# A graph layer on one core: rows in a ring of 66 tiles instead of six buffers, asked for earlier, and their places turned and spread at other times

## The chip, the cores and the metric

The kernel runs on one core of one Trainium2 chip. The metric is device microseconds of one launch. Before the change the median of three runs is 5410.82 us (5407.89 to 5411.46).

## The reference, cut to what matters

The reference is one attention layer over a graph of 12,500 nodes (128 features) and 412,500 edges, sorted by their second node, around a layer norm and a residual:

```python
h = relu(layernorm(x))
hmid = leaky_relu(concat([q[src], k[tgt], eh]) @ A1 + b1, 0.2)      # q, k, v from h; eh from the edge's 64 features
scores = leaky_relu(hmid @ A2 + b2, 0.2)                            # 8 heads
w = softmax(scores.mean(-1), axis=0)                                # over all edges
out = segment_sum(w[:, None] * v[tgt], src, num_segments=num_nodes)
y = x + gamma * normalize(h @ Wn + bn + out) + beta
```

The sum goes to the edge's first node (src), while the edges are sorted by the second. So each edge's row must be brought from one order into the other.

## The kernel before

**Chunks and blocks.** The edges are cut into four chunks (403 groups of 1024 edges: 121, 109, 98 and 75 groups). The nodes are cut into 98 blocks by their first node. In each chunk a block has room for a fixed number of tiles of 128 edges: 11, 10, 9 and 7. Tiles are worked on in quads of up to four, three quads for a block of the first three chunks, two for one of the last.

**First pass** (`first_stage`). For each group, SP loads the edge features, a window of the k and v table, and the edges' offsets in it (L769, L774, L777). Four times a group PE makes two tiles of rows (L809, L812), ACT copies them into a ring of 16 rows with their place in front (L792, L795), and POOL scatters each tile of 128 rows of 257 floats with an indirect DMA (L747) to the block's slots in a table in HBM. Two such tables are used in turn.

**Second pass** (`second_stage`). It goes through the blocks of the chunk before, in steps counted as half steps, two for each quad. For a block whose first quad is turned at half step t:

- `load` (L834, L837): SP loads the block's rows (tiles x 128 x 257 floats) into one of six buffers of 11 tiles, and the block's q rows (qw, five buffers). The time comes from `load_at`: 17 half steps ahead of t with three quads, 11 with two, but not before the block six earlier has been multiplied.
- `places` (L841): PE transposes the column of places into the PSUM bank t_bank. `put_places` (L846, L848), one half step later: ACT copies it to plT and stores it to HBM (pl_d). `spread_places` (L854): SP loads it back to all 128 partitions (pls, two buffers). With three quads these come at t - 9, t - 8 and t - 6, with two at t - 8, t - 7 and t - 5.
- `select` (L861): DVE makes sel_q from pls at t - 1. `turn` (L870, L873): PE transposes the rows and adds the node's q rows by sel_q. `steep` (L881, L882): ACT and DVE apply the leaky relu. `heads_of` to `exponentials` (L889 to L943): heads, scores, running maximum and weights.
- `weights` (L955) and `products` (L964), eleven half steps (LAG) after t: DVE makes a weighted selection for each tile and PE multiplies it with the v part of the rows into o_ps; `add_sums` (L973) adds that to the sums.

**What sets the order.** The program order of PE, DVE, ACT and SP is written out by hand. `at(when, turn, job)` puts each job into a half step and a rank in it. `interleave` mixes the first pass of a chunk with the second pass of the chunk before in proportion to their numbers of steps: 588 half steps in each of the first two mixtures, 594 in the third, and 414 of the last chunk alone behind it. The first pass of chunk 0 runs ahead of them with the work on the nodes. Each engine works in its order, so an instruction that waits holds all that stand behind it; SP's queue carries all loads.

I call the mixtures stages 1, 2 and 3 and the last chunk's second pass stage 4. At the start of each, the first load of rows waits until the last scatter of the chunk has landed.

Of the kernel before, what the change touches and what calls it, by code (L numbers as in the profile page):

```python
# [10 lines left out]
FP = mybir.dt.float32  # L11
# [3 lines left out]
U8 = mybir.dt.uint8  # L15
# [7 lines left out]
P = 128  # L23
# [10 lines left out]
QUAD = 4  # L34
LAG = 11

BUFS = 6

RROWS = 16

# [10 lines left out]
ROW = 2 * D + 1  # L51
# [18 lines left out]
def interleave(*jobs):  # L70

    jobs = [[g, max(n, 1), 0] for g, n in jobs]
    while jobs:
        job = min(jobs, key=lambda j: (j[2] + 0.5) / j[1])
        try:
            next(job[0])
            job[2] += 1
        except StopIteration:
            jobs.remove(job)


def some_steps(job, n):

    for _ in range(n):
        next(job, None)
        yield
# [25 lines left out]
def kernel(ctx: ExitStack, tc: tile.TileContext, n_edges, x, src, dst, ea, w_nv, w_qt, w_kt,  # L112
# [12 lines left out]
    nc = tc.nc  # L125
# [17 lines left out]
    most_tiles = max(ct for _, _, ct, _ in chunks)  # L143

    blocks = []
# [25 lines left out]
    def clear_ends(c):  # L171

        ct = chunks[c][2]
        k = min(SPARE, ct)
        for b in range(NTN):
            nc.sync.dma_start(out=tabs[c % 2][(b * ct + ct - k) * P:(b + 1) * ct * P, :].rearrange("(p j) r -> p (j r)", p=P),
                             in_=blank[:, 0:k * ROW])
            yield
# [13 lines left out]
    first = once.tile([P, P], FP, name="first")  # L192
# [225 lines left out]
    def clear_rest(c):  # L418

        ct = chunks[c][2]  # L420
        rest = ct - min(SPARE, ct)
        if rest > 0:
            turns = nc.values_load(trips[0:1, c:c + 1], min_val=0, max_val=NTN, skip_runtime_bounds_check_because=BECAUSE)
            with tc.For_i(0, turns, 1) as b:
                for j in range(rest):
                    nc.sync.dma_start(out=tabs[c % 2][ds(b * (ct * P) + j * P, P), :], in_=blank[:, 0:ROW])
# [84 lines left out]
    def ready(c):  # L511

        yield from count(c)
        yield from plan(c)
        yield from place_slots(c)

    def ready_steps(c):
        nt = chunks[c][1] * SUPER
        return _ceil(nt, 5 * STR) + 4 + 2 * _ceil(nt, STR)

    def ready_enough():

        return ready_steps(0) - 2 * _ceil(chunks[0][1] * SUPER, STR) + 2 * 2 * 8 + 1
# [146 lines left out]
    main = ctx.enter_context(ExitStack())  # L670
# [153 lines left out]
    def second_stage():  # L824


        rows_of, qws, plss, state = {}, {}, {}, {}
        state["s_ps"] = ps_s.tile([P, 512], FP, name="s_ps")
        nc.vector.memset(state["s_ps"], 0.0)

        def load(i):
            c, b, ct, _, _ = blocks[i]
            rows_of[i] = pb.tile([P, most_tiles, ROW], FP, name="rows_of")
            nc.sync.dma_start(out=rows_of[i][:, 0:ct, :],  # L834
                              in_=tabs[c % 2][b * ct * P:(b + 1) * ct * P, :].rearrange("(p j) r -> p j r", p=P))
            qws[i] = ps.tile([P, 3 * D], BF, name="qw")
            nc.sync.dma_start(out=qws[i], in_=q_tab.rearrange("(p t) d -> t p d", p=P)[b])  # L837
# [4 lines left out]

        def put_places(i):
            ct = blocks[i][2]
            plT = p3.tile([most_tiles, P], U8, name="plT")
            nc.scalar.activation(plT[:ct, :], t_bank[:ct, 0:P], AF.Copy)  # L846
            at = i % 4 * most_tiles
            nc.scalar.dma_start(out=pl_d[at:at + ct, :], in_=plT[:ct, :])  # L848
# [129 lines left out]
        def at(when, turn_, job, *args):  # L978
            plan_of.setdefault(when, []).append((turn_, len(plan_of[when]) if when in plan_of else 0, job, args))

        for i, (c, b, ct, nq, i0) in enumerate(blocks):
            t = 2 * i0
            at(load_at(i), 2, load, i)
            first = t - 9 if nq > 2 else t - 8
            at(first, 3, places, i)
            at(first + 1, 0, put_places, i)
            at(first + 3, 0, spread_places, i)
            at(t - 1, 3, select, i)
            for q in range(nq):
                at(t + 2 * q, 1, turn, i, q)  # L990
                at(t + 2 * q + 1, 0, steep, i, q)
            t += 2 * nq
            at(t - 1, 3, heads_of, i)
            at(t, 0, add_bias, i)
            at(t + 1, -1, by_slot, i)
            at(t + 1, -1, scores, i)
            at(t + 2, 2, spread_top, i)
            at(t + 2, 3, greatest, i)
            at(t + 3, 2, exponentials, i)
            at(t + 4, 3, add_weights, i)  # L1000
            t = 2 * i0 + LAG
            for q in range(nq):
                at(t + 2 * q - 1, 0, weights, i, q)
                at(t + 2 * q, 1, products, i, q)
            at(t + 2 * nq - 1, 0, add_sums, i)
        for when in range(min(plan_of), max(plan_of) + 1):
            for _, _, job, args in sorted(plan_of.get(when, []), key=lambda j: j[:2]):
                job(*args)
            yield

    def load_at(i):

        _, _, _, nq, i0 = blocks[i]
        t = 2 * i0 - (17 if nq > 2 else 11)
        if i >= BUFS:
            _, _, _, nq, i0 = blocks[i - BUFS]
            t = max(t, 2 * (i0 + nq - 1) + LAG)
        return t

    def all_sums():  # L1020

# [8 lines left out]
    def count_left():  # L1030

        nc.tensor.matmul(t_bank[:, 0:1], lhsT=ones, rhs=left, start=True, stop=True)
        nc.vector.tensor_scalar(trips[:, NC:NC + 1], t_bank[0:1, 0:1], 0.0, float(NG), op0=ALU.is_gt, op1=ALU.mult)

    def other_edges(most_of):

        with tc.tile_pool(name="others", bufs=1) as op, tc.tile_pool(name="others_ps", bufs=1, space=PSUM) as ops_:
            turns = nc.values_load(trips[0:1, NC:NC + 1], min_val=0, max_val=NG, skip_runtime_bounds_check_because=BECAUSE)
            with tc.For_i(0, turns, 1) as g:  # L1039
# [71 lines left out]
                with tc.For_i(0, NTN, 1) as b:  # L1111
# [8 lines left out]
                    nc.vector.tensor_add(a, a, bank[:, 0:D])  # L1120

    second = second_stage()
    ends = [load_at(c * NTN) for c in range(NC)]
    ends.append(2 * (blocks[-1][4] + blocks[-1][3]) + LAG)
    for c in range(NC + 1):
        jobs = []
        if c == NC:
            count_left()
        else:
            if c == 0:  # L1130
                clear_rest(c)
            jobs.append((first_stage(c), chunks[c][1] * halves))
        if c > 0:
            n = ends[c] - ends[c - 1]
            jobs.append((some_steps(second, n), n))
        if c == 0:
            jobs.append((chain(first_ready, ready(1)), ready_steps(0) - ready_enough() + ready_steps(1)))
        elif c + 1 < NC:
            jobs.append((ready(c + 1), ready_steps(c + 1)))
        if c + 1 < 2:  # L1140
            jobs.append((clear_ends(c + 1), NTN))
        if c == 0:
            with tc.manual_schedule(engines={ET.PE, ET.DVE, ET.Activation, ET.SP}):
                interleave(*jobs)
                for _ in node_steps:
                    pass
            clear_rest(1)
            setup.close()
            pb = main.enter_context(tc.tile_pool(name="pb", bufs=BUFS))
            ps = main.enter_context(tc.tile_pool(name="ps", bufs=5))  # L1150
            pw = main.enter_context(tc.tile_pool(name="pw", bufs=8))
            p3 = main.enter_context(tc.tile_pool(name="p3", bufs=1))
            ps_h = main.enter_context(tc.tile_pool(name="ps_h", bufs=2, space=PSUM))
            ps_s = main.enter_context(tc.tile_pool(name="ps_s", bufs=1, space=PSUM))
            ps_o = main.enter_context(tc.tile_pool(name="ps_o", bufs=1, space=PSUM))
        else:
            with tc.manual_schedule(engines={ET.PE, ET.DVE, ET.Activation, ET.SP}):
                interleave(*jobs)
# [88 lines left out]
```

## Time and profile before

| | us |
|---|---|
| median of three runs | 5410.82 (5407.89 to 5411.46) |
| the profiled execution | 5393.0 |
| its span, first to last instruction | 5391.3 |
| busy PE, DVE, ACT, POOL | 4218.1, 4204.3, 2160.8, 3379.1 |
| mean granted clock of TensorE | 0.921 |

| stage | what runs | us of the span | scatters |
|---|---|---|---|
| start and first pass of chunk 0 | nodes, places, scatters | 0 to 1455 | 968 |
| 1 | first pass of chunk 1, second of chunk 0 | 1456 to 2664 | 872 |
| 2 | first pass of chunk 2, second of chunk 1 | 2668 to 3765 | 783 |
| 3 | first pass of chunk 3, second of chunk 2 | 3770 to 4686 | 599 |
| 4 | second pass of chunk 3 | 4690 to 5299 | none |
| end | normalization and output | 5299 to 5391 | none |

How to read the lines of the profile below: PE is the matrix engine and PEld its weight loads; DVE, ACT, POOL and SP are the vector, scalar, GpSimd and sync engines; SPq is SP's queue of DMA issues. A line of waits, "A <- B: x, n, m", says that A stood idle for x us in n cases, at most m us, until B released it. A line of a timeline has the start, the duration, the engine, the line of the kernel and what is written from what. A DMA's duration there is the time to issue it, not to move the data.

### The profile page before, as it was taken

How to read it: one execution, taken by the hardware profiler on the slowest of the kernel's cores; microseconds unless marked ns; L12 is line 12 of the kernel's file. 1: busy time of each engine (PE TensorE's matmuls, PEld its weight loads, DVE VectorE, ACT ScalarE, POOL GpSimd, SP SyncE). 2: the span in 40 equal slices, each digit the busy share in tenths (PEclk: the TensorE clock that was granted, in tenths of full speed). 3: DMA queues.
4: the chain of work that ended last, by engine and by line, in shares of the span. 5: the costliest groups of instructions: out<-in, count | busy, mean ns of one | idle time of the engine just before them, and what ended most of it. 6: DMA issues, size and time to landing. Idle time of an engine off the chain costs nothing. (4 is left out here: it accounts for less than half of the span.)

```text
span 5391.3 us, 90152 instructions
## 1 busy us (share of the span) xinstructions
PE 4218.1 (78%) x26817; PEld 2951.6 (55%) x27160; DVE 4204.3 (78%) x13299; ACT 2160.8 (40%) x6046; POOL 3379.1 (63%) x3261
## 2 busy tenths in 40 slices
PE   4777766565588888998788888987888888878782
PEld 2344433333266666666566666665666666655551
DVE  7777754544378888888788988887877788799889
ACT  1344422222244444444344444443444444434333
POOL 0477777777677777777667777777666666500002
PEclk8788887777789999999999999999999999999996
DMA  8677765555489999888789999988899998755554
GB/s 244 201 234 228 230 196 162 169 164 167 162 262 290 280 280 282 279 281 281 251 257 284 289 284 282 282 286 260 263 284 280 276 287 284 242 194 193 190 194 164
DMA packets 609678, 1309.97 MB, mean 243 GB/s; under 512 B 117392, under 2 KB 371524, under 8 KB 571168
## 3 DMA queue, kind: packets, MB, share of 16 engines
q1 hardware_dynamic: 404312, 841.81, 53.1%
q0 software_dynamic: 154704, 424.26, 21.8%
q10 hardware_dynamic: 50168, 38.07, 2.2%
q8 instruction: 218, 3.57, 0.3%
q14 instruction: 276, 2.26, 0.1%
HBM read 782.14 MB, written 521.60 MB: 242 GB/s over the span
## 5 line engine op out<-in xcount | busy, mean ns | idle before, releaser
L747 POOL DMA_INDIRECT tab<-row,slots x3223 | 3343.9, 1038 | 1339.5 <-issue 702.8
L809 PE MATMUL row_ps<-w_ea,ea_t 128*128 128x256 f32 x3224 | 1105.0, 427 | 379.2 <-ACT row L795 311.5
L964 PE MATMUL o_ps<-rows_of,w 128*128 128x128 f32 x7252 | 1073.6, 287 | 127.9 <-DVE w L955 125.7
L964 PEld LDWEIGHTS o_ps<-rows_of,w 128*128 128x128 f32 x7252 | 954.8, 193 | 254.7 <-DVE w L955 199.7
L795 ACT ACTIVATE row<-row_ps 128x512 f32<-128x512 f32 x1612 | 939.6, 590 | 279.7 <-PE row_ps L812 215.7
L955 DVE TENSOR_SCALAR w<-iota_f,rows_of,score 128x128 f32<-128x128 f32 x3626 | 1037.2, 356 | 0.8 <-ACT score L938 0.8
L809 PEld LDWEIGHTS row_ps<-w_ea,ea_t 128*128 128x128 f32 x3224 | 577.9, 208 | 680.9 <-ACT row L795 397.7
L881 ACT ACTIVATE low<-h_ps 128x512 f32<-128x512 f32 (+3 forms) x1078 | 569.0, 528 | 848.7 <-PE h_ps L873 690.8
L873 PE MATMUL h_ps<-sel_q,qw 128*128 128x512 bf16 (+3 forms) x2891 | 753.7, 344 | 60.1 <-DVE sel_q L861 40.2
L882 DVE TENSOR_TENSOR rows_of<-h_ps,low 128x512 f32<-128x512 f32 (+3 forms) x1078 | 648.2, 601 | 134.7 <-ACT low L881 121.3
L812 PE MATMUL row_ps<-kv,sel 126*128 126x256 bf16 x3224 | 666.3, 290 | 1.5 <-DVE sel L785 1.5
L792 ACT ACTIVATE row<-place 128x4 f32<-128x4 bf16 x806 | 166.9, 207 | 1219.5 <-DMA tab<-row,slots 1195.7
L870 PE MATMUL h_ps<-ident,rows_of 128*128 128x128 f32 x3626 | 592.9, 279 | 0.0
L450 DVE TENSOR_TENSOR one<-bins_b,block 128x500 f16<-128x500 bf16 x646 | 301.5, 467 | 326.8 <-PE run L457 322.8
L812 PEld LDWEIGHTS <-sel 126*128 126x128 bf16 x3224 | 337.6, 105 | 279.3 <-issue 55.0
L870 PEld LDWEIGHTS h_ps<-ident,rows_of 128*128 128x128 f32 x3626 | 433.1, 143 | 102.2 <-issue 39.5
L503 DVE TENSOR_REDUCE num<-run 128x5 f32<-128x500 f32 x646 | 433.4, 671 | 11.8 <-PE run L457 11.8
L861 DVE TENSOR_SCALAR sel_q<-pls,part 128x1408 bf16<-128x1408 uint8 (+3 forms) x392 | 330.6, 843 | 108.5 <-DMA pls<-pl_d 108.0
L1174 POOL TENSOR_TENSOR xt<-xt,affine 128x640 f32<-128x640 f32 (+1 forms) x20 | 32.7, 1649 | 608.2 <-DMA xt<-in_x 595.4
L873 PEld LDWEIGHTS <-qw 128*128 128x128 bf16 x3234 | 314.9, 99 | 160.7 <-issue 54.6
L889 PE MATMUL s_ps<-rows_of,a_sb 128*32 128x352 f32 (+3 forms) x3136 | 292.2, 444 | 117.2 <-DVE rows_of L882 116.1
L457 PE MATMUL run<-one,rest_b 128*128 128x500 f16 x642 | 268.9, 419 | 145.1 <-DVE num L503 143.9
(195 smaller groups left out, 4161.9 us busy)
## 6 DMA issues: line engine op xcount, KB each, us to landing
rows_of<-tab SPq DMA_DIRECT2D x98, 1413.5 KB
rows_of<-tab SPq DMA_DIRECT2D x98, 1285.0 KB
rows_of<-tab SPq DMA_DIRECT2D x98, 1156.5 KB
ea_t<-in_ea SPq DMA_DIRECT2D x403, 256.0 KB
rows_of<-tab SPq DMA_DIRECT2D x98, 899.5 KB
tab<-row,slots POOLq DMA_INDIRECT x3223
offs<-off_d SPq DMA_DIRECT2D x403, 126.0 KB
tab<-blank SPq DMA_DIRECT2D x196, 257.0 KB
```

Of the source, the lines that this page charges most:

```text
L503: nc.vector.tensor_reduce(num, strips[:, :, :m].rearrange("p b m -> p m b"), AX.X, ALU.max)
L747: i = nc.gpsimd.indirect_dma_start(out=tabs[c % 2][:, :], out_offset=bass.IndirectOffsetOnAxis(ap=slots[c][t // (8 * STR)][:m, t % (8 * ST ...
L795: nc.scalar.activation(row[:, :, 1:ROW], bank, AF.Copy)
L809: nc.tensor.matmul(bank[:, :, 0:D], lhsT=ea_g[:, ts(k, P)], rhs=w_ea, start=True, stop=False, skip_group_check=True)
L812: nc.tensor.matmul(bank[:, b, :], lhsT=sel[:, ts(b * halves + k, P)], rhs=kv, start=False, stop=True, skip_group_check=True)
L861: nc.vector.tensor_scalar(sel[:, 0:n], plss[i][:, 0:n], part1, None, op0=ALU.is_equal)
L870: nc.tensor.matmul(h_ps[:, ts(j, P)], lhsT=rows_of[i][:, q * QUAD + j, 1:D + 1], rhs=ident, is_transpose=True, start=j == 0, stop=False, s ...
L873: nc.tensor.matmul(h_ps[:, 0:m * P], lhsT=qws[i][:, ts(k, D)], rhs=plss[i][:, q * QUAD * P:(q * QUAD + m) * P], start=False, stop=k == 2, ...
L881: nc.scalar.activation(low, h_ps, AF.Copy, scale=SLOPE)
L882: nc.vector.tensor_max(rows_of[i][:, q * QUAD:q * QUAD + m, 1:D + 1], h_ps.rearrange("p (j e) -> p j e", j=m), low.rearrange("p (j e) -> p ...
L955: nc.vector.tensor_scalar(w, iota_f, rows_of[i][:, t, 0:1], state["score", i][:, t:t + 1], op0=ALU.is_equal, op1=ALU.mult)
L964: nc.tensor.matmul(state["o_ps"][:, 0:D], lhsT=w, rhs=rows_of[i][:, t, D + 1:ROW], start=t == 0, stop=t == ct - 1)
```

## The change

The six buffers become one tile of 66 tiles, used as a ring: each block takes as many tiles as it has (11, 10, 9 or 7) behind the block before, and starts again at 0 where it doesn't fit. The memory is the same, 6 x 11 tiles. A list worked out ahead says from which half step the space of a block is free. `load_at` asks for rows 19 half steps ahead of t with three quads and 17 with two, or when the space is free. In the first two chunks a block's space is that of the block six earlier, as before; in the third it is seven, in the last nine.

The places are turned (`places`) at t - 11 for all blocks and copied and stored (`put_places`) at t - 10, plT having two buffers instead of one. They are spread (`spread_places`) at t - 6 with three quads, as before, and at t - 7 with two. The stages get 588, 588, 590 and 420 half steps. No instruction is added or removed.

```diff
-BUFS = 6
+RING = 66
...
+        held = pb.tile([P, RING, ROW], FP, name="rows_of")
...
-            rows_of[i] = pb.tile([P, most_tiles, ROW], FP, name="rows_of")
-            nc.sync.dma_start(out=rows_of[i][:, 0:ct, :],
+            rows_of[i] = held[:, place_of[i]:place_of[i] + ct, :]
+            nc.sync.dma_start(out=rows_of[i],
...
-            plT = p3.tile([most_tiles, P], U8, name="plT")
+            plT = p3.tile([most_tiles, P], U8, name=f"plT{i % 2}")
...
-            first = t - 9 if nq > 2 else t - 8
+            first = t - 11
             at(first, 3, places, i)
             at(first + 1, 0, put_places, i)
-            at(first + 3, 0, spread_places, i)
+            at(first + (5 if nq > 2 else 4), 0, spread_places, i)
...
+    place_of, owner_of, free_at = [], [None] * RING, []
+    for i, (_, _, ct, _, _) in enumerate(blocks):
+        at = place_of[-1] + blocks[i - 1][2] if i else 0
+        if at + ct > RING:
+            at = 0
+        place_of.append(at)
+        free_at.append(max((2 * (blocks[j][4] + blocks[j][3] - 1) + LAG for j in owner_of[at:at + ct] if j is not None),
+                           default=None))
+        owner_of[at:at + ct] = [i] * ct
+
     def load_at(i):
-        _, _, _, nq, i0 = blocks[i]
-        t = 2 * i0 - (17 if nq > 2 else 11)
-        if i >= BUFS:
-            _, _, _, nq, i0 = blocks[i - BUFS]
-            t = max(t, 2 * (i0 + nq - 1) + LAG)
-        return t
+        t = 2 * blocks[i][4] - (19 if blocks[i][3] > 2 else 17)
+        return t if free_at[i] is None else max(t, free_at[i])
...
-            pb = main.enter_context(tc.tile_pool(name="pb", bufs=BUFS))
+            pb = main.enter_context(tc.tile_pool(name="pb", bufs=1))
```

## The prediction, made before the changed kernel was run

> **What bounds the kernel now.** I read the page first, then busy times by stage, then the waits of each stage, then a few microseconds of the last stage in order of time.
>
> ```profile
> span 5391.3 us, 90152 instructions
> PE 4218.1 (78%) x26817; PEld 2951.6 (55%) x27160; DVE 4204.3 (78%) x13299; ACT 2160.8 (40%) x6046; POOL 3379.1 (63%) x3261
> DMA  8677765555489999888789999988899998755554
> 1456.00:2664.00 1208.00, 1055.92 (x7042) 765.73 (x7138) 1016.74 (x3122) 516.56 (x1321) 920.86 (x872) 0.96 0.89 277
> 2668.00:3765.00 1097.00, 965.03 (x6648) 711.64 (x6746) 943.13 (x3022) 503.60 (x1367) 827.83 (x783) 0.98 0.89 277
> 3770.00:4686.00 916.00, 802.60 (x5683) 596.08 (x5783) 726.66 (x2360) 433.98 (x1243) 622.38 (x599) 0.99 0.90 277
> ```
>
> The windows are stages 1, 2 and 3 (second pass of chunks 0, 1, 2 beside the first pass of chunks 1, 2, 3). Their columns are length, busy PE, PEld, DVE, ACT and POOL with instruction counts, granted clock, DMA share and GB/s. PE, DVE and DMA are each at 79 to 90%, and no share says which one binds. The waits do.
>
> ```profile
> POOL tab L747 <- issue: 199.0, 649, 0.6
> ```
>
> This is stage 1: between two scatters POOL stands 199.0/649 = 0.307 us waiting for nothing. So a scatter takes 920.86/872 + 0.307 = 1.363 us in stage 1, and 872 of them 1188 of its 1208 us. Stage 2 gives 827.83 + 783 x 0.307 = 1068 of 1097. **POOL binds stages 1 and 2**, with 20 and 29 us to spare, a good part of which is the turn from one chunk to the next. In stage 3 the same sum is 622.38 + 599 x 0.307 = 806 of 916: there POOL does not bind.
>
> ```profile
> PE h_ps L873 <- DVE sel_q L861: 39.6, 48, 1.8
> PE o_ps L964 <- DVE w L955: 28.5, 58, 1.2
> PE t_bank L841 <- DMA rows_of<-tab: 23.2, 12, 3.4
> DVE sel_q L861 <- DMA pls<-pl_d: 100.4, 79, 2.8
> SPq L854 <- DMA pl_d<-plT: 539.0, 98, 8.6
> ...
> SPq L854 <- DMA pl_d<-plT: 1682.4, 311, 11.1
> ```
>
> **Stage 3** (waits from 3774 to 4684): PE is idle for 916 - 802.6 = 113 us. 39.6 of them wait for sel_q, which DVE could not make because the places (pls) had not landed (100.4 us of DVE), and 23.2 for rows. The last two rows, SP's in stage 3 and in the whole run, are the cause: SP stands 539.0 us, 98 times, at the spread of the places until their store has landed, and all later loads stand behind it.
>
> ```profile
> 4700.00:5260.00 560.00, 447.69 (x3441) 320.63 (x3487) 503.84 (x1883) 224.02 (x661) 0.00 (x0) 0.99 0.58 191
> DVE acc L973 <- PE o_ps L964: 45.5, 81, 3.3
> PE t_bank L841 <- DMA rows_of<-tab: 57.4, 51, 3.4
> SPq L834 <- PE o_ps L964: 384.5, 92, 6.6
> SPq L854 <- DMA pl_d<-plT: 30.8, 22, 5.7
> ```
>
> **Stage 4** (the last chunk alone): DVE is busy 503.84 of 560 us, and 45.5 of its 56.2 idle us are add_sums waiting for PE. PE is late because the transposes of the places wait for rows (57.4). SP waits 384.5 us for products to give back a buffer, so rows are asked for only 11 half steps ahead, three before the transposes. One block in order of time:
>
> ```profile
> 4989.67 0.33 SPq L834 DMA_DIRECT2D rows_of<-tab  x1
> 4994.47 0.27 PE L841 MATMUL t_bank<-ident,rows_of 128*7 128x128 f32 x1 [0.79 <-DMA rows_of<-tab]
> 5247.07 0.34 DVE L973 SCALAR_TENSOR_TENSOR acc<-acc,fade_of,o_ps 128x128 f32<-128x128 f32 x1
> 5252.42 0.35 DVE L973 SCALAR_TENSOR_TENSOR acc<-acc,fade_of,o_ps 128x128 f32<-128x128 f32 x1
> L973 DVE SCALAR_TENSOR_TENSOR acc<-acc,fade_of,o_ps x94: 336/348/349, 4701.6 to 5258.5; 128x128 f32<-128x128 f32 x94
> ```
>
> A load takes 4.80 us from issue to its first reader, which stood 0.79 us. Two blocks that no load held up are 5.35 us apart. 94 blocks in 560 us are 5.96 us each, and DVE's own work is 503.84/94 = 5.36.
>
> **The change part by part.** No instruction comes or goes; the change moves DMA issues, transposes and the two small copies behind them. I work in half steps: 560/94/4 = 1.49 us in stage 4, 916/594 = 1.54 in stage 3.
>
> (a) **Ring of 66 tiles, loads at 19 and 17.** In chunks 0 to 2 the lead goes from 17 to 19 half steps and the transposes go from 9 to 11 ahead, so 8 half steps lie between load and transposes, as before. The space is free at 21 ahead (chunks 0 and 1) or earlier, so the load is not held for it unless SP runs over two half steps ahead of PE. In the last chunk nine blocks of 7 tiles fit instead of six: the space of a block is free at 23, the load goes out at 17 (was 11), the transposes come at 11 (was 8). Six half steps or 8.9 us stand where three or 4.5 us stood, against the 4.80 us of the load. Only the 57.4 us can hide there, and they go. What DVE gets back is what it waited for: 45.5 of the 56.2 idle us. What is late next is DVE itself, at 5.36 us a block; PE's 447.69/94 = 4.76 fits under it. I take **48 us** (bounds 0, if another wait takes the place, and 56; a loss is excluded, since DVE, which sets the pace, gets no work). The new wait is on SP: qw has five buffers, so its load at 17 ahead stands until the turn of the block five earlier, which is at 18, is done. Queued behind it are the spread of an older block's places, needed six half steps after it is asked, and the next rows, with 8.9 us of lead. Neither is late by that.
>
> The entry into stage 4:
>
> ```profile
> PE t_bank L841 <- DMA rows_of<-tab: 7.8, 2, 7.3
> SPq L834 <- DMA tab<-row,slots: 43.6, 4, 15.1
> ```
>
> The first row is 4670 to 4715: the first transposes waited 7.3 us for rows that may be asked for only when the last scatter has landed. With three half steps (4.5 us or more) more lead I count **7**. The second row, whole run, is SP waiting for that last scatter at the four turns; it stays, as the data demand it. Six half steps move from stage 3 into stage 4 and two are added at the start of stage 1: at about 1.4 us, and with stage 3 shorter by four, this costs **2**.
>
> (b) **Transposes at 11, copy and store at 10, spread at 6 (7 in the last chunk).** Store to spread grows from two half steps to four (three).
>
> ```profile
> 4304.25 0.27 ACTq L848 DMA_DIRECT2D pl_d<-plT  x1
> 4309.89 0.33 SPq L854 DMA_DIRECT2D pls<-pl_d  x1
> 4995.07 0.27 ACTq L848 DMA_DIRECT2D pl_d<-plT  x1
> 4997.98 0.32 SPq L854 DMA_DIRECT2D pls<-pl_d  x1
> ```
>
> Store issue to spread, where SP stood waiting for it, is 5.64 us in stage 3 and 2.91 in stage 4. Four half steps are 6.2 us and three are 4.5: SP's 539.0 us of stage 3 go nearly whole, spreads go out five half steps (7.7 us) before sel_q, and sel_q's wait (39.6 us of PE) and the rows' (23.2) go with them. The bound above is 62.8 us. From below there is DMA:
>
> ```profile
> 3000.00:3250.00 250.00, 223.48 (x1536) 164.53 (x1556) 218.82 (x700) 117.61 (x322) 192.94 (x181) 0.99 0.92 285
> 4170.00:4180.00 10.00, 9.09 (x67) 7.01 (x68) 8.66 (x28) 5.25 (x15) 6.28 (x6) 1.00 1.02 322
> ```
>
> No 250 us had a share over 0.92; at that the 916 us become 916 x 0.90/0.92 = 896, a gain of 20. Ten microseconds reached 1.02. POOL's floor, 806, is not reached by either bound. I take **40**, the middle, since PE's waits lie on the engine with the least slack while DMA has some. If DMA has none, it is 0. The Trainium skill speaks against this part: "DMA: Bandwidth & Descriptors", section "Anatomy of one DMA", gives about 2.0 us fixed for one DMA, at which a 1 KB store lands within the old two half steps and moving the spread frees nothing. The row's 5.64 us disagrees. By the page only the rows' 23.2 us would be left of stage 3, and the sum would be 76 instead of 93.
>
> In stages 1 and 2 SP is freed too, but POOL sets their time: **0** (bounds: 48 gained, which is all of POOL's spare time, or a loss by longer scatters, below). The transposes go behind products on PE instead of behind other steps; the two copies stay on even half steps of ACT. The second plT buffer takes a wait from ACT, which is busy only 433.98 of 916 us: nothing. Cover for all of it: rows land at least three half steps before they are read; if that cover is gone, each block costs the 0.6 us (5.96 - 5.36) of today's stage 4.
>
> **Sum:** 48 + 7 - 2 + 40 = 93 us off. The profiled execution took 5393.0 us beside its span of 5391.3, and would take 5300. It lies 17.8 us (0.33%) below the median of the runs, 5410.8, so the forecast for the median is 5411 - 93 = **5318**.
>
> **The rivals.** (A) DMA is full in stage 3: its waits only change their names, and 53 remain: 5358. For it speaks the share of 0.90 with PE, DVE and POOL each below it; against it the ten microseconds at 322 GB/s.
>
> (B) Stage 3 opens fully (62.8) and DVE runs without a gap in stage 4 (56): 56 + 7 - 2 + 63 = 124, so 5287. For it: a DMA share of 0.97 would do (0.90 x 916/853). Against it: w and s_ps waits remain and other work queues closer. The Trainium skill, same page, section "Where 436 GB/s comes from", puts the limit of a core's HBM at about 358 GB/s, on which 277 leave the room that B needs; the trace's best ten microseconds, 322, do not contradict it, the share of 1.02 in them does.
>
> (C) In stage 4 the new wait at qw takes the place of the old one: 7 - 2 + 40 = 45 off, 5366. Against it: it is pinned at 18 where the old one was at 11.
>
> (D) Slower: the scatter lengthens. SP's loads, no longer metered by the hold, lie beside the scatters in another order.
>
> ```profile
> L747 POOL DMA_INDIRECT tab<-row,slots x3223: 932/969/2074, 175.7 to 4685.6; - x190
> ```
>
> The median scatter is 0.969 us, the mean of stages 1 and 2 1.057; where POOL binds, 1655 scatters pay the difference. The gain is eaten from 93/1655 = 56 ns on (mean 1.113). If the excess doubles, it costs 1655 x 0.088 = 146: 5464. Against it: bytes per scatter stay the same.
>
> (E) The change does nothing, because SP is only held at other waits and rows land as late as before: 5411.
>
> **How the numbers follow.** Forecast 0.44, A 0.25, B 0.12, C 0.06, D 0.08, E 0.05. Faster by over 0.2% (10.8 us, about what a measurement of this kernel can tell from no change) is the forecast, A, B and C, 0.87; within it is E, 0.05; slower is D, 0.08. The range of 5265 to 5385 holds A, B and C and part of POOL's spare time; D, E and the far end of B, under 2 in 10, are left out.
>
> **What would show it.** Right: in stage 4 add_sums follows at 5.4 us and "DVE acc <- PE o_ps" falls below 5 us; SP's wait at the spread falls from 1682 us in all (539.0 in stage 3) to a few hundred; sel_q's wait in stage 3 is below 15 us and that stage takes about 876 us; stages 1 and 2 stay at 1208 and 1097 within 15. Wrong: stage 3 at 916 with DMA at 0.90 (A); SP's time before the load of stage 4 turns up at qw with DVE still idle (C); scatters above 1.1 us (D).

## The result and the profile after

| | before | after |
|---|---|---|
| median, same chip | 5409.35 us (5401.93 to 5411.46, 4 runs) | 5320.1 us (5314.46 to 5323.74, 4 runs) |
| profiled execution / span | 5393.0 / 5391.3 us | 5319.57 / 5317.9 us |

The ratio is 0.9836, 95% interval 0.9819 to 0.9854: **faster by 1.6%**, 89 us. 5318 was forecast. Counted from the first load of rows of each chunk to that of the next, the two profiled executions differ so (us):

| | start | stage 1 | stage 2 | stage 3 | stage 4 and end | span |
|---|---|---|---|---|---|---|
| before | 1455.3 | 1211.1 | 1101.2 | 921.2 | 702.4 | 5391.3 |
| after | 1458.2 | 1204.8 | 1117.4 | 888.4 | 649.1 | 5317.9 |
| difference | +2.9 | -6.3 | +16.2 | -32.8 | -53.3 | -73.4 |

The page of the changed kernel:

```profile
span 5317.9 us, 90276 instructions
PE 4224.0 (79%) x27160; PEld 2957.4 (56%) x27160; DVE 4195.2 (79%) x13299; ACT 2152.6 (40%) x6046; POOL 3423.2 (64%) x3261
DMA  8677765555489888898888888888788999967764
```

DVE does the same work in a span that is 73 us shorter, and POOL, with the same 3261 instructions, is busy 44 us longer: a first sign that the scatters got longer. The stages 1 to 4 of the changed kernel, columns as before (length, PE, PEld, DVE, ACT, POOL, clock, DMA share, GB/s):

```profile
1460.00:2662.00 1202.00, 1053.76 (x7123) 761.81 (x7123) 1015.10 (x3111) 521.15 (x1320) 923.72 (x872) 0.97 0.88 279
2666.00:3778.00 1112.00, 982.37 (x6746) 717.27 (x6746) 944.48 (x3022) 503.61 (x1367) 854.79 (x784) 0.97 0.86 273
3782.00:4666.00 884.00, 794.35 (x5745) 594.14 (x5746) 718.35 (x2347) 419.25 (x1236) 634.52 (x598) 0.98 0.90 288
4671.00:5225.00 554.00, 489.68 (x3743) 357.91 (x3741) 538.78 (x2031) 238.84 (x704) 9.24 (x6) 0.99 0.68 209
```

In stage 4 DVE is busy 538.78 of 554 us (97%, was 503.84 of 560, 90%). In stage 2 one scatter takes 854.79/784 = 1.090 us; it was 827.83/783 = 1.057. Waits of the changed kernel, first stage 1, then stage 3, then stage 4, then SP in the whole run:

```profile
POOL tab L747 <- issue: 188.9, 612, 2.1
...
DVE sel_q L862 <- DMA pls<-pl_d: 49.1, 28, 5.1
PE o_ps L965 <- DVE w L956: 45.0, 74, 1.3
...
PE h_ps L874 <- DVE sel_q L862: 29.3, 14, 4.5
SPq L855 <- DMA pl_d<-plT: 362.8, 81, 9.0
...
DVE acc L974 <- PE o_ps L965: 1.5, 2, 1.1
PE t_bank L842 <- DMA rows_of<-tab: 1.0, 1, 1.0
SPq L855 <- DMA pl_d<-plT: 274.4, 78, 8.6
SPq L838 <- PE s_ps L922: 91.9, 59, 2.3
...
SPq L769 <- PE row_ps L812: 923.6, 202, 13.8
SPq L835 <- PE o_ps L965: 767.9, 143, 12.6
SPq L855 <- DMA pl_d<-plT: 717.9, 205, 9.0
```

The gap between two scatters is 188.9/612 = 0.309 us, as before. In stage 3 PE's wait for rows has left the list, the wait for sel_q is 29.3 us (39.6 before), and SP still stands 362.8 us at the spread. In stage 4 add_sums no longer waits (1.5 for 45.5), and the new wait at qw is there (91.9 us of SP) and delays nobody. In the whole run SP's hold at the spread fell from 1682.4 to 717.9 us, but two others stand ahead of it now: 923.6 at the edge features (673.3 before) and 767.9 at the space for rows (391.3 before). Two rows for add_sums in stage 4 and for the scatters:

```profile
L974 DVE SCALAR_TENSOR_TENSOR acc<-acc,fade_of,o_ps x102: 331/339/348, 4676.2 to 5222.4; 128x128 f32<-128x128 f32 x102
L747 POOL DMA_INDIRECT tab<-row,slots x3223: 930/972/2287, 176.3 to 4666.2; - x190
```

101 intervals in 546.2 us are 5.41 us a block, for 5.96 before.

### The profile page after: what moved, and what is told of

It reads as the page before. It is cut to its first block, busy times and chain, and to the rows that moved or that the text cites. A ratio compares the mean times of both kernels' runs of the same rounds, so it can differ in the third digit from the quotient of the medians.

```text
span 5317.9 us, 90276 instructions
## 1 busy us (share of the span) xinstructions
PE 4224.0 (79%) x27160; PEld 2957.4 (56%) x27160; DVE 4195.2 (79%) x13299; ACT 2152.6 (40%) x6046; POOL 3423.2 (64%) x3261
## 5 line engine op out<-in xcount | busy, mean ns | idle before, releaser
L747 POOL DMA_INDIRECT tab<-row,slots x3223 | 3389.2, 1052 | 1274.9 <-issue 724.4
L874 PE MATMUL h_ps<-sel_q,qw 128*128 128x512 bf16 (+3 forms) x3234 | 773.9, 349 | 37.3 <-DVE sel_q L862 34.0
L897 ACT ACTIVATE z<-s_ps,b_col 128x352 f32<-128x352 f32 (+3 forms) x392 | 199.0, 508 | 553.8 <-PE s_ps L890 553.8
L862 DVE TENSOR_SCALAR sel_q<-pls,part 128x1408 bf16<-128x1408 uint8 (+3 forms) x392 | 329.0, 839 | 61.8 <-DMA pls<-pl_d 61.4
```

The costliest lines, as they stand in the source:

```text
L747: i = nc.gpsimd.indirect_dma_start(out=tabs[c % 2][:, :], out_offset=bass.IndirectOffsetOnAxis(ap=slots[c][t // (8 * STR)][:m, t % (8 * ST ...
L862: nc.vector.tensor_scalar(sel[:, 0:n], plss[i][:, 0:n], part1, None, op0=ALU.is_equal)
L874: nc.tensor.matmul(h_ps[:, 0:m * P], lhsT=qws[i][:, ts(k, D)], rhs=plss[i][:, q * QUAD * P:(q * QUAD + m) * P], start=False, stop=k == 2, ...
```

## The experiments

**Theory.** Stage 4 gains because rows and places both come earlier there; stage 3 gains what SP's hold gives back; stage 2 loses by another order of the loads beside the scatters, which POOL's chain has to bear. **Rivals.** One of the two parts does it all; the hold at the spread isn't what stage 3 waited for; the longer scatters have to do with something else than the order of the loads.

Ratios are against the kernel before, run on the same chip in turn. The first four ran on a chip on which every kernel, the one before too, took some 13% longer in all; the profiles show it in the start and stages 1 to 3 and not in stage 4. They are compared with each other only.

| run | before | run, median | ratio (95%) |
|---|---|---|---|
| ring_only | 6140.22 | 6158.48 | 1.0038 (1.0019 to 1.0058) |
| places_only | 6140.22 | 6124.44 | 0.9975 (0.9954 to 0.9997) |
| spread_close | 6140.22 | 6077.01 | 0.9905 (0.9873 to 0.9937) |
| first_ahead | 6140.22 | 6065.53 | 0.9891 (0.9858 to 0.9924) |
| after_again | 5349.28 | 5301.24 | 0.9902 (0.9881 to 0.9924) |
| ring_last | 5349.28 | 5311.45 | 0.9924 (0.9908 to 0.9940) |
| spread_close_2 | 5349.28 | 5309.89 | 0.9920 (0.9899 to 0.9942) |
| first_ahead_2 | 5349.28 | 5229.51 | 0.9773 (0.9756 to 0.9791) |
| four_ahead | 5375.99 | 5268.31 | 0.9806 (0.9791 to 0.9821) |
| two_ahead | 5375.99 | 5242.12 | 0.9760 (0.9744 to 0.9776) |
| phase_2 | 5375.99 | 5270.89 | 0.9812 (0.9797 to 0.9827) |
| before_ahead | 5375.99 | 5338.60 | 0.9932 (0.9916 to 0.9948) |

Stages of the runs on the second and third chip, in us, with the mean of one scatter in stage 2. The kernel before was not profiled on these two chips, and the changed kernel's stage 3 alone differs by 18 us between two chips (888.4 and 870.3), so differences of stages across chips are rough. The mean of a scatter repeats better: 1.091 and 1.090 in the two profiles of the changed kernel.

| run | stage 1 | stage 2 | stage 3 | stage 4 and end | scatter |
|---|---|---|---|---|---|
| after_again | 1203.9 | 1120.5 | 870.3 | 648.2 | 1.090 |
| ring_last | 1202.1 | 1108.7 | 902.2 | 646.6 | 1.083 |
| spread_close_2 | 1200.1 | 1113.0 | 896.4 | 645.0 | 1.082 |
| first_ahead_2 | 1190.5 | 1071.5 | 861.1 | 649.5 | 1.036 |
| four_ahead | 1188.3 | 1100.8 | 875.1 | 650.8 | 1.091 |
| two_ahead | 1198.7 | 1077.9 | 856.5 | 648.9 | 1.058 |
| phase_2 | 1210.2 | 1084.0 | 874.0 | 646.9 | 1.072 |
| before_ahead | 1201.0 | 1083.6 | 902.4 | 695.5 | 1.059 |

### One part alone: ring_only and places_only

ring_only is the changed kernel with the places of before:

```diff
-            first = t - 11
+            first = t - 9 if nq > 2 else t - 8
-            at(first + (5 if nq > 2 else 4), 0, spread_places, i)
+            at(first + 3, 0, spread_places, i)
-            plT = p3.tile([most_tiles, P], U8, name=f"plT{i % 2}")
+            plT = p3.tile([most_tiles, P], U8, name="plT")
```

places_only is the kernel before with the places of the first three chunks moved, and two plT buffers:

```diff
-            first = t - 9 if nq > 2 else t - 8
+            first = t - 11 if nq > 2 else t - 8
-            at(first + 3, 0, spread_places, i)
+            at(first + (5 if nq > 2 else 3), 0, spread_places, i)
-            plT = p3.tile([most_tiles, P], U8, name="plT")
+            plT = p3.tile([most_tiles, P], U8, name=f"plT{i % 2}")
```

> The changed kernel with the places as before the change: turned at t-9 (t-8 with two quads), spread two half steps behind their store, one plT buffer; the ring and the loads at 19 and 17 stay. Theory (the ring opens stage 4, the distance from store to spread opens stage 3): stage 4 and the end as in the changed kernel (649 us from the first load of the last chunk, 702 before), stage 3 near 915 (921 before, six less for four half steps fewer), SP held over 500 us at the spread in stage 3; about 5350 in all. Rival (the longer lead of the loads opens stage 3 as well): stage 3 near 888, about 5320 in all.

> The kernel before with the places of the three-quad chunks turned at t-11 and spread at t-6, and two plT buffers; six buffers, loads at 17 and 11, and the last chunk's places as before. Theory: stage 3 falls from 921 to about 894, stage 4 and the end stay at 702; about 5380 in all. Rival (the loads' lead opens stage 3): nothing, 5409. What could go wrong: the transposes now come six half steps behind their load instead of eight, so PE may wait for rows; up to 23 us more in stage 3 than today.

The ring alone is 0.4% slower, the places alone are 0.25% faster. Stage 3 takes 1044.2 us with the ring alone, 1016.1 with the places alone and 1015.1 in spread_close, which has both: there the places do it. Stage 2's scatters take 1.082 us with the ring alone and 1.051 with the places alone: the longer scatters come with the ring. Stage 4 and the end take 699.4 us with ring_only, where 649 was expected, and 696.8 with places_only, which leaves the last chunk as it was; spread_close and first_ahead, which have both parts there, took 650.1 and 647.7 on the same chip. A window of 500 us of stage 4 in ring_only, with its waits of DVE and SP, shows what took the place of the old wait:

```profile
5500.00:6000.00 500.00, 412.55 (x3123) 291.97 (x3164) 452.82 (x1709) 193.99 (x599) 0.00 (x0) 1.00 0.66 196
DVE sel_q L862 <- DMA pls<-pl_d: 40.8, 46, 2.6
SPq L855 <- DMA pl_d<-plT: 377.6, 86, 8.0
```

DVE is busy 452.82 of 500 us (91%) as in the kernel before: the rows are early, but the places are stored as late as ever, and now sel_q waits for them. So in stage 4 the lead of the ring and the earlier places of the last chunk give some 50 us together, and the lead without the places next to nothing (699.4 against 696.8 with neither). The earlier places of the last chunk without the lead were not run.

### The last chunk's places alone, and the spread closer: ring_last and spread_close

ring_last, against the changed kernel:

```diff
-            first = t - 11
+            first = t - 9 if nq > 2 else t - 11
-            at(first + (5 if nq > 2 else 4), 0, spread_places, i)
+            at(first + (3 if nq > 2 else 4), 0, spread_places, i)
```

spread_close and spread_close_2, against the changed kernel:

```diff
-            at(first + (5 if nq > 2 else 4), 0, spread_places, i)
+            at(first + 3, 0, spread_places, i)
```

> The changed kernel with the spread back at two half steps behind its store (t-8 with three quads, t-8 with two), all else as changed. Theory (SP standing at the spread makes the loads behind it late): SP held over 500 us in stage 3 again, stage 3 back to about 910, about 5340 in all. Rival (the hold itself is harmless; sel_q only needed its places asked for earlier than t-6): the spread goes out earlier than in the changed kernel, sel_q's wait in stage 3 falls from 49 us to under 10, and stage 3 is at 888 or below, 5320 or less in all.

> The changed kernel with the places of the three-quad chunks as before the change (turned at t-9, spread at t-6, two half steps behind their store); the last chunk keeps t-11 and t-7, and the ring and the loads stay. Theory (stage 4 needs the rows and the places both earlier, stage 3 the distance from store to spread): stage 4 and the end 649 us as in the changed kernel, not 699 as with the ring alone; stage 3 some 25 us longer than in the changed kernel. Rival (the last chunk's gain was the loads' alone, and the ring alone missed it for another reason): 690 or more.

> The changed kernel with the spread two half steps behind its store, beside the changed kernel on the same chip. The first run of it had the spread out earlier and SP held 240 us at it in stage 3 with sel_q's wait gone. If the hold itself costs, its stage 3 is at least 15 us longer than in the changed kernel; if only late places cost, within 10 us of it.

> The changed kernel as it is, as the reference for the runs beside it: the ratio to the kernel before on the same chip is 0.983 to 0.990; stage 4 and the end 649 us. It also tells whether stage 2's scatters are longer than before the change every time (1.090 against 1.057 us in the first profile) or only in that profile. If the change lengthens them, stage 2 takes 10 us or more longer than in the kernel before here too.

Stage 4 is open in both (646.6 and 645.0). Stage 3 tells them apart. Its waits in ring_last:

```profile
DVE sel_q L862 <- DMA pls<-pl_d: 93.8, 62, 3.4
PE h_ps L874 <- DVE sel_q L862: 38.4, 33, 3.0
PE t_bank L842 <- DMA rows_of<-tab: 1.2, 1, 1.2
SPq L855 <- DMA pl_d<-plT: 558.5, 97, 9.5
```

and in spread_close_2:

```profile
PE t_bank L842 <- DMA rows_of<-tab: 29.3, 17, 3.1
DVE sel_q L862 <- DMA pls<-pl_d: 1.9, 4, 0.8
PE h_ps L874 <- DVE sel_q L862: 0.3, 1, 0.3
SPq L855 <- DMA pl_d<-plT: 504.6, 96, 8.4
```

ring_last loses nothing to rows and 38.4 us to the places; spread_close_2 asks for the places earlier, loses nothing to them and 29.3 us to the rows that stand behind the spread. It is one hold with two ends, and it costs: beside the changed kernel on the same chip stage 3 is 26 us longer in spread_close_2 and 32 in ring_last. The two PE waits together are 62.8 us before, 39.6 in ring_last, 29.6 in spread_close_2, 29.3 after and 17.3 in after_again; the stage takes 921.2, 902.2, 896.4, 888.4 and 870.3. **What PE no longer waits goes with what the stage gains**: 23, 33, 34 and 46 us of waits against 19, 25, 33 and 51. This is no full account: the first and fourth of the five times are from the first comparison's chip, all stages but the first have four half steps fewer (some 6 us), and PE's wait for w rose meanwhile (28.5 us before, 46.4 after).

after_again is the changed kernel on another chip: 0.9902, 48 us, where the first comparison gave 89. The changed kernel differs little (5301 and 5320); the kernel before took 5349 here and 5409 there. Why was not settled.

### Why stage 2 got longer: one, two and four steps ahead, and phase_2

The turn from one chunk to the next comes first. At the turn into stage 3 of the changed kernel PE waits for the edge features, and POOL for ACT:

```profile
POOL tab L747 <- ACT row L795: 52.6, 31, 14.2
PE row_ps L809 <- DMA ea_t<-in_ea: 17.7, 1, 17.7
```

The load of ea stands in SP's queue behind the first load of rows, which waits for the last scatter. So one step of the new first pass was run ahead of it:

```diff
             with tc.manual_schedule(engines={ET.PE, ET.DVE, ET.Activation, ET.SP}):
+                if c < NC:
+                    next(jobs[0][0])
                 interleave(*jobs)
```

That is first_ahead and first_ahead_2 against the changed kernel, and before_ahead against the kernel before. two_ahead and four_ahead call next two and four times. phase_2 runs nothing ahead, but begins the stages 2 to 4 two half steps earlier:

```diff
-    ends = [load_at(c * NTN) for c in range(NC)]
+    ends = [load_at(c * NTN) - (2 if c else 0) for c in range(NC)]
```

> The changed kernel with one step of each chunk's first pass put ahead of the second pass's first load of rows at the turn from stage to stage, so that the edge loads of the new chunk don't stand on SP behind the wait for the last scatter. Theory (that wait costs its whole length at each turn): POOL's gap at the turns falls from 11.7, 12.3 and 14.2 us to about 1, three times 10 to 12 us less, about 5285 in all. Rival (the time comes back, because the second pass then starts later against the first): between 5310 and 5320.

> One step of each chunk's first pass ahead of the second pass's first load, beside the changed kernel on the same chip. Theory: POOL's gap at the three turns falls from 12 to 14 us to under 3, and the time is 25 to 35 us below the changed kernel's. Rival: the first rows of the second pass come later by as much, within 10 us of the changed kernel.

On the first chip first_ahead could not be told from spread_close: its scatters of stage 2 were shorter (1.035 us for 1.085), the stage was not (1326.5 us for 1324.0), and POOL stood 312 us of it waiting for ACT's rows. On the second it gave 72 us over the changed kernel on the same chip where the turns had promised 25 to 35. Against after_again stage 1 gained 13 us and stage 3 nine, but stage 2 gained 49, and 43 of these are in the scatters (854.93 us for 784 became 812.11). One thing that differs is at which wait SP stands in stage 2. Before, after, and first_ahead_2:

```profile
SPq L854 <- DMA pl_d<-plT: 588.4, 96, 9.4
```

```profile
SPq L835 <- PE o_ps L965: 534.7, 79, 12.0
```

```profile
SPq L769 <- PE row_ps L812: 616.4, 92, 12.0
```

In all three SP stands over 530 us of stage 2 at one wait; the change only moved the place, from the spread to the space for rows in the ring. What follows that wait goes out in one burst, rows first. SP's queue after:

```profile
3306.42 0.33 SPq L835 DMA_DIRECT2D rows_of<-tab  x1
3306.80 0.43 SPq L838 DMA_DIRECT2D qw<-q_tab  x1
3308.11 0.33 SPq L769 DMA_DIRECT2D ea_t<-in_ea  x1
...
3309.80 0.39 SPq L855 DMA_DIRECT2D pls<-pl_d  x1
3317.06 0.36 SPq L835 DMA_DIRECT2D rows_of<-tab  x1
```

and in first_ahead_2, where ea comes first:

```profile
3300.33 0.33 SPq L769 DMA_DIRECT2D ea_t<-in_ea  x1
...
3301.87 0.35 SPq L835 DMA_DIRECT2D rows_of<-tab  x1
...
3311.92 0.33 SPq L769 DMA_DIRECT2D ea_t<-in_ea  x1
```

Stage 2 has 98 groups beside 98 blocks, so this order, and with it the place of the first pass against the second, stands for the whole stage. Two things had changed together, the turn and this place. The last four runs part them.

> B is the time of the kernel before on the same chip. The changed kernel with four steps of the new first pass run at each turn before the second pass goes on, where first_ahead ran one. Four steps are one group of edges, so within a stage the loads of rows and of ea stand in SP's queue in the order of the changed kernel (rows, then ea about 1 us later), while the turns gain as with one step. If that order lengthens the scatters of stage 2 (changed kernel 1.091 us in the mean, one step ahead 1.036), they take 1.08 to 1.10 here, stage 2 takes 1100 to 1115 us, and the run is 70 to 105 us below B. If running ahead itself is what helps, the scatters are at 1.03 to 1.05, stage 2 at 1070 to 1080, and the run is 115 to 130 us below B.

> The changed kernel with two steps of the new first pass run ahead at each turn. The ea loads then go out 4 to 6 us ahead of the rows, against 1.5 us with one step ahead. If rows ahead of the smaller loads in one burst lengthen the scatters, these take 1.03 to 1.05 us in stage 2, that stage takes 1065 to 1080 us and the run is 115 to 135 us below B. If only the exact distance of one step helps, the scatters are at 1.06 to 1.10 and the run is 75 to 105 us below B.

> The changed kernel with the stages 2 to 4 begun two half steps earlier: the last two half steps of the older blocks go into the next stage, so that rows are loaded two half steps behind the ea load of the same turn and not beside it. Nothing runs ahead. If the order of rows and ea sets the length of the scatters, they take 1.03 to 1.05 us in stage 2, stage 2 takes 1070 to 1090 us and the run is 85 to 125 us below B. If it doesn't, they stay at 1.08 to 1.10, and the run is 45 to 90 us below B, as the changed kernel.

> The kernel before with one step of the new first pass run ahead at each turn, and nothing else. If the turns' gain (POOL stands about 12 us at each turn of the changed kernel, and 1 to 8 with one step ahead) doesn't need the change, the run is 25 to 50 us below B, with scatters of stage 2 at or below the 1.057 us of the kernel before. If the hold of SP at the spread of the places sets the order of the loads, so that a step ahead moves nothing, it is within 15 us of B.

Stage 2 of four_ahead, two_ahead, phase_2 and before_ahead; the last busy time with its count is POOL's, nearly all scatters:

```profile
2639.80:3740.60 1100.80, 976.10 (x6664) 713.62 (x6761) 946.77 (x3026) 502.44 (x1373) 856.09 (x785) 0.98 0.85 277
```

```profile
2657.00:3734.90 1077.90, 962.40 (x6644) 710.69 (x6738) 955.64 (x3022) 510.19 (x1368) 829.44 (x784) 0.98 0.88 282
```

```profile
2663.50:3747.60 1084.10, 965.45 (x6702) 710.69 (x6800) 949.69 (x3031) 498.26 (x1379) 841.52 (x785) 0.99 0.87 281
```

```profile
2657.00:3740.70 1083.70, 966.72 (x6652) 716.23 (x6751) 944.51 (x3017) 504.83 (x1372) 831.42 (x785) 0.97 0.90 281
```

- **four_ahead** is the control: turns improved, order as after (ea a median 0.94 us behind rows, after 0.93). Its scatters are as long as after (1.091), so running ahead as such does not shorten them. Stage 2 is 16.6 us shorter than after, on another chip; POOL's gap at the turn into it is 1.0 us instead of 12.3. The whole run gained 108 us, a little over the 70 to 105 that the theory of the order gave.
- **two_ahead** and **phase_2** change the order, phase_2 without any step ahead: scatters of 1.058 and 1.072, below every kernel with rows 0.9 us ahead of ea (1.082 to 1.091), but not at the 1.03 to 1.05 expected. So it is shown that the place of the first pass against the second sets the length of the scatters, with the same bytes. That it acts through the order of rows and ea in SP's queue does not fit the sizes: with the next ea a median 5.6, 6.9, 8.4 and 8.7 us behind the rows (before_ahead, two_ahead, phase_2, first_ahead_2) the means are 1.059, 1.058, 1.072 and 1.036, in no simple order. And the kernel before, with ea a median 1.07 us behind the rows (upper quartile 1.93), had 1.057. The next paragraphs show what fits better.
- **before_ahead** gains 37 us: the turns' gain needs nothing of the change, and the scatters stay at 1.059.

**What runs beside the long scatters.** DVE makes two selections that compare bytes: sel for the first pass (L785, a median 0.74 us) and sel_q for the second (L862 after the change, 0.88). Sort the scatters of stage 2 by whether one of them is running in the scatter's first 0.9 us (none is shorter than 0.93):

| run | without a selection | with one |
|---|---|---|
| before | 0.991 us (541) | 1.203 us (243) |
| after | 0.982 (566) | 1.376 (218) |
| four_ahead | 0.979 (566) | 1.381 (219) |
| phase_2 | 0.989 (623) | 1.401 (161) |
| two_ahead | 0.978 (520) | 1.217 (263) |
| before_ahead | 0.995 (535) | 1.204 (249) |
| first_ahead_2 | 0.992 (604) | 1.184 (180) |

All 128 scatters over 1.3 us of the changed kernel have a selection beside them. Two neighbours from the burst shown above, 4.7 and 6.0 us behind its load of rows:

```profile
3311.13 0.97 POOL L747 DMA_INDIRECT tab<-row,slots  x1 [0.30 <-issue]
3312.41 1.27 POOL L747 DMA_INDIRECT tab<-row,slots  x1 [0.30 <-ACT row L795]
3312.82 0.75 DVE L785 TENSOR_SCALAR sel<-offs,third 126x1024 bf16<-126x1024 uint8 x1
```

So the long scatters go with DVE's selections, and the others take 0.98 to 1.00 us whatever the order of the loads. The place of the first pass against the second shifts the selections against each other and against POOL. sel_q starts a median 1.8 us ahead of sel in after and four_ahead (1.091), 0.8 ahead in first_ahead_2 (1.036), 1.0 behind in phase_2 (1.072), 2.6 behind in two_ahead (1.058) and 3.9 behind in the kernel before (1.057). No run moved the selections alone, so that they are the cause is argued from seven profiles and not tested, and why these distances give these means stays open.

two_ahead (0.9760) and first_ahead_2 (0.9773) are the fastest; their intervals overlap, and they were not run on one chip.

## Why the prediction was right, and where it was not

- **(a) Stage 4, 48, entry 7, moved half steps -2: right in size and mechanism.** 53 forecast, 53.3 in the profile. The first transposes wait 1.0 us (7.3 before), blocks follow at 5.41 us, and the bound is DVE, as the step said. Rival C is out: SP stands at qw and DVE is not idle. The runs add that the lead alone gives next to nothing there (ring_only); the step named the places' move to 11 too, but gave the gain to the load.
- **(b) Stage 3, 40: near in size, wrong in a premise.** 33 in the first profile, of which some 6 are the four half steps that moved on into stage 4, and 51 in the second, on another chip than the kernel before. The rows' 23.2 us went. "SP's 539.0 us of stage 3 go nearly whole" failed: 362.8 stayed, and sel_q's wait stayed at 29.3 us, not under 15. The step compared four half steps of program order (6.2 us) with the landing of the store (5.64 us). But SP does not walk in half steps: it runs through its queue until something holds it, so it came to the spread earlier than the program order says: in stage 3 of the changed kernel it was free for the spread a median 1.1 us after the store's issue (86 blocks), not 6.2. The lower bound of 20 was no bound either: "no 250 us had a share over 0.92" is a misreading, the 250 us from 3820 us on had 0.94. Rival A (DMA full) is out: the stage got shorter at a share of 0.90 (288 GB/s for 277).
- **(c) Stages 1 and 2, 0: the step that failed**, with 16 us lost in stage 2 and 6 gained in stage 1. The zero held POOL's time per scatter to be unchanged; it rose from 1.057 to 1.091 us in stage 2, and to 1.090 in after_again. Rival D had the longer scatters, and they came in one of the two stages that POOL binds, not at the 1.113 in both that would have eaten the gain. Its reason, another order of SP's loads, is not what the traces show: the long scatters are those that run beside DVE's selections. "Bytes per scatter stay the same" was true and no argument: the place of the other work alone moves the mean between 1.036 and 1.091. Rival E's first half was right too (SP is held at other waits), without its conclusion.
- **The sum.** The profile gives -73 for the 93 forecast, and the medians -89; the 16 us between them are the kernel before, whose profiled execution lay 0.3% under its median, where the changed kernel's lay on it. That 5318 met 5320.1 so closely is in part luck: stage 2's loss is hidden in that difference, and on the second chip the gain was 48 us, half of the sum.
- The Trainium skill, "DMA: Bandwidth & Descriptors", section "Anatomy of one DMA", has about 2.0 us as the fixed cost of a DMA; its heading limits this to DMAs issued from GpSimd, and the prediction applied it to a store that ACT issues. The changed kernel's stage 4 shows 2.94 and 5.46 us for that store of places (below), so the figure does not fit it. By the rule stage 3 would have gained 23 us; it gained 33 and 51. That its sum of 76 lies near the profile's 73 is due to the loss in stage 2.

## What to carry to other kernels

In each of these kernels the queue that runs ahead stood at some wait; moving a DMA later in program order did not remove the hold but handed it to the next gate, so ask which gate comes next and which loads stand behind it. Where an engine that issues transfers of its own sets the pace, compare the mean of its instructions by stage before and after, even if their bytes are unchanged, and sort the long ones by what the other engines do at that time before blaming the transfers. And when a chunk's first load has to wait for data, see that loads which need not wait stand ahead of it: it was worth 37 us to the kernel before, and with the shift of the two passes that came along 72 to the changed one.

## What the runs showed of the hardware

**A small store landed later behind a large load.** Stage 4 of the changed kernel, in order of time:

```profile
4942.26 0.42 SPq L835 DMA_DIRECT2D rows_of<-tab  x1
...
4944.26 0.27 ACTq L849 DMA_DIRECT2D pl_d<-plT  x1
...
4949.58 0.27 ACTq L849 DMA_DIRECT2D pl_d<-plT  x1
4949.72 0.32 SPq L855 DMA_DIRECT2D pls<-pl_d  x1
...
4952.52 0.32 SPq L855 DMA_DIRECT2D pls<-pl_d  x1
```

The store at 4944.26, issued 2.0 us after a load of rows (7 x 128 x 257 floats), is waited for until 4949.72, 5.46 us. The next, 7.3 us after that load, takes 2.94. Of the stage's 98 stores, the 32 issued over 4.5 us after the last load of rows have a median of 2.94 us from store to spread (at most 3.19), the 60 issued 0.3 to 2.5 us after one 4.94 (2.94 to 6.10).

**A scatter's own time goes with what DVE does beside it.** Between 2900 and 3600 us (stage 2), the 65 scatters of the changed kernel that start 4.5 to 6 us after a load of rows was issued take 1.38 us in the mean, and those up to 1.5 us after it 0.98; in first_ahead_2 the same two groups take 1.03 and 1.02, and in spread_close_2, whose stage mean is 1.082, 0.99 and 1.18. So the distance to the load doesn't decide. Of the 65, the 47 with a selection of DVE in their first 0.9 us take 1.53 and the other 18 take 0.99. The Trainium skill, "Perfetto Trace Analysis", section "DMA Instruction — SWDGE (GPSIMD)", says that the time shown for such an instruction ends when the descriptors are written and not when the data have moved, and that the DMA engines may begin on them before that if more are made than fit in the descriptor buffer. A full buffer behind slow DMA engines could lengthen it too, but it should then lengthen the 18 as well; no run here shows the buffer.

**Chips differ.** The kernel before took 5349, 5376, 5409 and 6140 us on the chips of these comparisons, so only ratios on one chip can be set beside each other. On the slowest of them the granted clock of its runs was 0.86 to 0.88, on the others 0.92 to 0.93; no run shows whether that is the whole reason.
